# Layer 1 of a two-layer Mamba kernel: x turned by VectorE and laid out through DRAM instead of transposed on TensorE, with a new step order

## The chip, the cores and the metric

The kernel runs on one core of a Trainium2 chip, as one launch. The metric is the device time in microseconds, the median of several runs. Before the change the median of 3 runs is 8054.4 us (8048.22 to 8063.68).

## The reference

The input x is 2 images of 64 x 64 positions with 256 channels, in f32. Two layers follow each other, each as `x = x + layer(groupnorm(x))`. Layer 0 is a Mamba block with a scan over time. It runs in both directions along rows and along columns. Layer 1, which the change concerns, applies a Mamba-2 block four times (two stacked layers, each first along the columns and then along the rows). It treats every row or column of 64 positions as a sequence:

```python
def _mamba2(x, Win, Wconv, bconv, dt_bias, A_log, D, gn_w, Wout):
    zxbcdt = x @ Win
    z = zxbcdt[..., :DIN]
    xBC = silu(_causal_conv(zxbcdt[..., DIN:DIN + CONVDIM], Wconv, bconv))
    xh = xBC[..., :DIN].reshape(b, l, NHEADS, HEADP)
    Bm, Cm = xBC[..., DIN:DIN + DSTATE], xBC[..., DIN + DSTATE:]
    dt = softplus(zxbcdt[..., -NHEADS:] + dt_bias)
    A = -exp(A_log)
    y = _ssd(xh, dt, A, Bm, Cm) + rev(_ssd(rev(xh), rev(dt), A, rev(Bm), rev(Cm)))
    y = y + D[None, None, :, None] * xh
    return _rmsnorm(y.reshape(b, l, DIN) * silu(z), gn_w) @ Wout

# in _ssd:
    scores = einsum('bln,bsn->bls', Cm, Bm)[..., None] * decay * dt[:, None, :, :]
    return einsum('blsh,bshp->blhp', scores, xh)
```

DIN is 512, DSTATE 64, there are 8 heads of 64 channels and 4 convolution taps. Each application reads `x + _mamba2(_rmsnorm(x, w), ...)`.

## The kernel before

Channels lie on the 128 partitions and positions run along the free dimension. Both images stay in SBUF during layer 1 (`U[0]` and `U[1]`). Layer 1 is cut into 128 blocks: 4 calls (columns, rows, columns, rows) x 2 images x 16 blocks of 4 sequences, that is 256 positions per block (`TB`). `seq_view` gives a block its positions: contiguous for rows, strided for columns.

For one block the steps are these. `norm_squares`, `norm_total`, `norm_mean`, `norm_factor` and `norm_scale` make the RMS norm `xn`, 2 tiles of 128 channels by 256 positions. `x_proj` 0 and 1, `bc_proj`, `z_proj` 0 and 1 and `dt_proj` multiply `xn` with pieces of the weight `w_in` on TensorE. The 512 x channels are 4 tiles of 128 (`c`), two for each `x_proj`. `conv_start` (ScalarE) and `conv_taps` (VectorE, L1151) are the causal convolution, with the taps of each channel from `cols`. `dt_bias`, `dt_log` and `dt_sum` make softplus: an addition on VectorE (L1245), three activations on ScalarE (absolute value, exponential, logarithm) and a combination on VectorE (L1255). `dt_turn` transposes dt, and `factors` turns it into decay factors per head and position, writes them to DRAM (L1272) and reads them back broadcast over the partitions as `spread` (L1280). `decay_after` (L1290) and `decay_before` (L1296) make the decay matrices of both directions by two scans each on VectorE. `silus` activates x, z, B and C. `scores`, `scores_twice`, `weights` and `mix` form the 64 x 64 mixing matrices of each head, the last two on GpSimd. `outputs` multiplies them with x on TensorE, and for that x has to lie with positions on the partitions, as `xt`: `x_transpose` (L1332) does this with 8 transposes of 128 x 128 on TensorE into PSUM, and `x_copy` with 2 copies on ScalarE into SBUF. `gated` (L1410), `out_squares`, `out_total` (L1419), `out_mean`, `out_factor`, `out_proj`, `out_scale` (`res`, L1446) and `residual` (L1461) finish the block. In call 3 `y_load` (L1457) fetches the original input of the block, which `residual` adds before it stores the result (L1464).

The order is written out by hand in the table `STEPS`. Step n of block i is issued at the time 100 x i + the number in the table. All steps of all blocks, and the steps of `WEIGHTS` and `NORM`, are sorted by that time and emitted in this order:

```python
    return [
        (period * i + step[0], first + i, n, getattr(thing, step[1]), step[2:])
        for i, thing in enumerate(things)
        for n, step in enumerate(steps)
    ]
```

The numbers are no durations; only the order that they give counts. Since a block's last step stands at 533, some six blocks are in work at once. Compute instructions are pinned to this order, so each engine works through a fixed queue and waits at its head until the inputs of the next instruction are there. All DMAs of layer 1 go out on SP's queue, in order as well, though the framework may place them earlier or later among each other. PSUM has 7 banks for the blocks (`bank()`), which go round among the projections, scans, transposes, outputs and sums; a step that asks for one waits until an earlier user has been read. In SBUF the pools `one`, `two` and `three` hold one to three copies of a tile.

The weights of the four calls are loaded by `Weights.load` and scaled on VectorE by `scale_in` and `scale_out`; `decay_rates` makes `neg_a`. Image 1 is normalised during the first blocks (`NORM`).

Of the kernel before, what the change touches and what calls it, by code (L numbers as in the profile page):

```python
# [34 lines left out]
FAR = 1e35  # L35
UC = CT // 2
PARTS = P // TAPS
SPAN = L + TAPS - 1
WIDE = SB * SPAN
TURN = 1000  # L40
# [181 lines left out]

STEPS = (
    (0, "norm_squares"),
    (67, "norm_total"),
    (94, "norm_mean"),
    (104.4, "norm_factor"),
    (110.5, "norm_scale"),
    (149.4, "dt_proj"),
    (155.6, "x_proj", 0),  # L230
    (176.9, "conv_start", 0),
    (181.3, "bc_proj"),
    (184.4, "dt_bias"),
    (203.1, "bc_conv_start"),
    (206.9, "x_proj", 1),
    (207, "conv_taps", 0),
    (208.4, "dt_log"),
    (210.1, "conv_start", 1),
    (220.5, "dt_sum"),
    (226.2, "dt_turn"),  # L240
    (230.1, "factors"),
    (244.2, "z_proj", 1),
    (246.3, "conv_taps", 1),
    (249.4, "z_proj", 0),
    (274.9, "silus"),
    (292.8, "x_transpose", 0),
    (307.9, "x_copy", 0),
    (320.5, "scores"),
    (332.5, "scores_twice"),
    (348.9, "x_transpose", 1),  # L250
    (360, "weights", 0),
    (360.1, "weights", 1),
    (366.2, "decay_after", 0),
    (367.5, "decay_before", 0),
    (370.8, "decay_after", 1),
    (374.6, "x_copy", 1),
    (379, "mix", 0),
    (386.6, "decay_before", 1),
    (418.1, "mix", 1),
    (421.1, "outputs"),  # L260
    (433.8, "gated"),
    (445.2, "out_squares"),
    (458.9, "out_total"),
    (460.1, "out_mean"),
    (477, "out_proj"),
    (492.8, "out_factor"),
    (503.2, "out_scale"),
    (505, "y_load"),
    (533, "residual"),
)  # L270


# [1 line left out]
    (-1500, "load"),  # L274
    (10, "scale_in", 0),
    (20, "scale_in", 1),
    (200, "decay_rates"),
    (240, "diag_skip"),
    (300, "scale_out", 0),
    (330, "scale_out", 1),  # L280
# [748 lines left out]
def layer1(tc, k, d, U, kept, out):  # L1029
# [7 lines left out]
    with ExitStack() as ctx:  # L1037
# [4 lines left out]
        three = ctx.enter_context(tc.tile_pool(name="l1_three", bufs=3))  # L1042
        ps = ctx.enter_context(tc.tile_pool(name="l1_ps", bufs=7, space=PSUM))
        ps_one = ctx.enter_context(tc.tile_pool(name="l1_ps_one", bufs=1, space=PSUM))
        dram = ctx.enter_context(tc.tile_pool(name="l1_dram", bufs=3, space=bass.MemoryType.DRAM))
        pin = tc.keep_in_program_order

        k.more(nc, one)
# [17 lines left out]
        class Weights:  # L1066
# [97 lines left out]
        class Block:  # L1164
# [41 lines left out]
            def conv_start(self, h):  # L1206
                if not hasattr(self, "conv"):
                    self.conv = two.tile([P, CT, TB], F32, name="conv")
                for j in (1, 0):
                    c = 2 * h + j  # L1210
                    last_tap(self.conv[:, c, :], half_of(self.px[h], j), self.w.cols[:, c, :])

            def conv_taps(self, h):
                parts = [(self.conv[:, 2 * h + j, :], half_of(self.px[h], j), self.w.cols[:, 2 * h + j, :]) for j in range(2)]
# [46 lines left out]
            def factors(self):  # L1261
                a = factors[self.i % 2]
                for way, ls in enumerate((steps_up, steps_down)):
# [3 lines left out]
                        AF.Exp,  # L1267
                        scale=self.w.neg_a,
                    )
                rows = dram.tile([2, 2, NPAIR, NH, L], F32, name="factor_rows")  # L1270
                for q in range(NPAIR):
                    nc.sync.dma_start(  # L1272
                        out=rows[:, :, q].rearrange("e w h l -> h e w l"), in_=a[q * NH : (q + 1) * NH]
                    )
                self.spread = []
                for way in range(2):
                    to = three.tile([P, NPAIR, NH * L], F32, name="spread")
# [46 lines left out]
                pin(nc.scalar.preload_act_table_set(LOG_EXP))  # L1324


            def x_transpose(self, q):
                self.pt = getattr(self, "pt", {})
                self.pt[q] = bank()
                for c in range(CT):  # L1330
                    pin(
                        nc.tensor.transpose(  # L1332
                            self.pt[q][:, c * P : (c + 1) * P],
                            self.xh[:, c, q * P : (q + 1) * P],
                            k.ident,
                        )
                    )

            def x_copy(self, q):
                if not hasattr(self, "xt"):  # L1340
                    self.xt = two.tile([P, NPAIR, NH, DI // NH], F32, name="xt")
                act(self.xt[:, q].rearrange("p h e -> p (h e)"), self.pt[q], AF.Copy)


            def scores(self):
# [20 lines left out]

            def weights(self, q):
                self.weight = getattr(self, "weight", {})
                w = two.tile([P, NH, L], F32, name=f"weight{q}", tag=f"weight{q}")
                pin(  # L1370
                    nc.gpsimd.tensor_mul(
                        w,
                        self.score[:, q, :].unsqueeze(1).to_broadcast([P, NH, L]),
                        self.dt[:, q, :].unsqueeze(2).to_broadcast([P, NH, L]),
                    )
                )
                pin(nc.gpsimd.tensor_add(w, w, self.w.diag_d))
                self.weight[q] = w
# [1 line left out]


            def mix(self, q):
                self.mixes = getattr(self, "mixes", {})
                self.mixes[q] = two.tile([P, NH, L], F32, name=f"mix{q}", tag=f"mix{q}")
                decay = self.decay[q].rearrange("p (h l) -> p h l", l=L)
                pin(nc.gpsimd.tensor_mul(self.mixes[q], decay, self.weight[q]))


            def outputs(self):
# [3 lines left out]
                for q in range(NPAIR):  # L1393
                    for hd in range(NH):
                        for e, py in enumerate(self.py):
                            rows = slice(e * L, (e + 1) * L)
                            matmul(
                                py[(hd % 2) * L : (hd % 2 + 1) * L, hd // 2, q, :],
                                self.xt[rows, q, hd, :],
                                self.mixes[q][rows, hd, :],  # L1400
                                q == 0 and hd < 2,
                                q == NPAIR - 1 and hd >= NH - 2,
                            )
# [11 lines left out]
                act(self.sq2, self.yg, AF.Square)  # L1415

            def out_total(self):
                half = one.tile([P, 2, TB], F32, name="half2")
                pin(nc.gpsimd.tensor_add(half, self.sq2[:, 0:2, :], self.sq2[:, 2:4, :]))  # L1419
# [134 lines left out]
```

## Time and profile before

| what | value |
|---|---|
| median of 3 runs | 8054.4 us |
| time of the profiled execution | 8063.64 us |
| its span | 8061.9 us |
| first weight load of layer 1 | at 5973.63 us |
| busy in the span: TensorE matmul, VectorE, ScalarE, GpSimd | 7580.3, 7404.4, 7187.3, 6926.5 us |
| mean granted TensorE clock | 0.991 |
| DMA mean rate over the span | 141 GB/s |

The span runs from the first to the last instruction of the profiled execution, and the execution's own time lies 1.7 us above it. Busy time is the time in which an engine had an instruction running. In rows of groups and of the timeline, PE is the TensorE matmul, PEld its weight load, DVE is VectorE, ACT is ScalarE, POOL is GpSimd and SP the queue that issues the DMAs; L12 is line 12 of the kernel. An f32 matmul appears as two records, a transpose as one. Names are those of the program's tiles; every PSUM bank of `bank()` is called `ps_mm`.

### The profile page before, as it was taken

How to read it: one execution, taken by the hardware profiler on the slowest of the kernel's cores; microseconds unless marked ns; L12 is line 12 of the kernel's file. 1: busy time of each engine (PE TensorE's matmuls, PEld its weight loads, DVE VectorE, ACT ScalarE, POOL GpSimd, SP SyncE). 2: the span in 40 equal slices, each digit the busy share in tenths (PEclk: the TensorE clock that was granted, in tenths of full speed). 3: DMA queues.
4: the chain of work that ended last, by engine and by line, in shares of the span. 5: the costliest groups of instructions: out<-in, count | busy, mean ns of one | idle time of the engine just before them, and what ended most of it. 6: DMA issues, size and time to landing. Idle time of an engine off the chain costs nothing. (4 is left out here: it accounts for less than half of the span.)

```text
span 8061.9 us, 165546 instructions
## 1 busy us (share of the span) xinstructions
PE 7580.3 (94%) x62162; PEld 6487.4 (80%) x62162; DVE 7404.4 (92%) x6547; ACT 7187.3 (89%) x12867; POOL 6926.5 (86%) x3912
## 2 busy tenths in 40 slices
PE   7999999999999999999999999999979999999999
PEld 6888887888777778878887788888768888888887
DVE  6999999999999999999999999999988888888887
ACT  6999999999999989999999999999978888888887
POOL 6999999999998989999999999999867776677777
PEclk9999999999999999999999999999999999999999
DMA  5555556556555556555555555565532222222333
GB/s 173 165 163 161 165 161 169 165 166 168 161 169 163 163 158 172 163 166 159 161 165 162 175 166 164 168 169 172 152 105 67 68 78 68 76 70 68 82 102 93
DMA packets 703597, 1140.70 MB, mean 141 GB/s; under 512 B 121552, under 2 KB 269008, under 8 KB 701264
## 3 DMA queue, kind: packets, MB, share of 16 engines
q1 hardware_dynamic: 687296, 1110.54, 48.7%
q10 hardware_dynamic: 15504, 19.58, 0.8%
q8 instruction: 493, 8.08, 0.4%
q14 instruction: 304, 2.49, 0.1%
HBM read 1069.12 MB, written 60.69 MB: 140 GB/s over the span
## 5 line engine op out<-in xcount | busy, mean ns | idle before, releaser
L898 POOL TENSOR_TENSOR prod<-prod,c_row 128x1024 f32<-128x1024 f32 x1280 | 3011.3, 2368 | 420.5 <-DVE prod L887 250.3
L520 PE MATMUL ps_y<-ident,prod 128*128 128x128 f32 x16384 | 2129.5, 276 | 190.8 <-POOL prod L898 178.3
L520 PEld LDWEIGHTS ps_y<-ident,prod 128*128 128x128 f32 x16384 | 1828.5, 141 | 465.3 <-POOL prod L898 275.5
L868 POOL TENSOR_TENSOR b<-dtx,b_row 128x1024 f32<-128x1024 f32 x832 | 1960.1, 2370 | 22.5 <-DVE ps_h L887 11.2
L513 ACT ACTIVATE b<-dt,neg_a 128x512 f32<-128x512 f32 x2432 | 1591.5, 710 | 38.2 <-DVE ps_h L887 36.4
L513 ACT ACTIVATE scaled<-dtxt,bt 128x256 f32<-128x256 f32 x3328 | 1434.3, 496 | 80.8 <-PE ps_h L520 75.2
L887 DVE TENSOR_TENSOR_SCAN prod<-b,ps_h 128x1024 f32<-128x1024 f32 x640 | 1453.3, 2279 | 49.2 <-PE ps_h L520 40.3
L887 DVE TENSOR_TENSOR_SCAN prod<-ps_h,b 128x1024 f32<-128x1024 f32 x640 | 1437.2, 2272 | 57.5 <-ACT dbc L513 34.6
L887 DVE TENSOR_TENSOR_SCAN ps_h<-b,ps_h 128x1024 f32<-128x1024 f32 x576 | 1305.2, 2276 | 2.9 <-PE ps_h L516 1.9
L513 ACT ACTIVATE ps_h<-dt,neg_a 128x512 f32<-128x512 f32 x1664 | 1145.8, 689 | 147.1 <-DVE prod L901 60.7
L1064 PE MATMUL ps_mm<-xn,w_in 128*128 128x256 f32 x4608 | 1113.6, 383 | 0.0
L901 DVE TENSOR_TENSOR prod<-ps_h,c_row 128x1024 f32<-128x1024 f32 x768 | 931.3, 1220 | 123.6 <-PE ps_y L520 56.7
L1064 PEld LDWEIGHTS ps_mm<-xn,w_in 128*128 128x128 f32 x4608 | 849.1, 191 | 100.2
L520 PE MATMUL ps_h<-ident,scaled 128*128 128x128 f32 x6656 | 890.7, 276 | 36.2 <-DVE prod L887 22.4
L520 PEld LDWEIGHTS ps_h<-ident,scaled 128*128 128x128 f32 x6656 | 741.1, 141 | 179.6 <-ACT scaled L513 66.1
L516 PE MATMUL ps_h<-diag,dtxt 128*128 128x128 f32 x6144 | 771.9, 279 | 40.4 <-DVE prod L887 22.9
L516 PEld LDWEIGHTS ps_h<-diag,dtxt 128*128 128x128 f32 x6144 | 718.1, 192 | 88.6 <-DVE prod L887 53.8
L1151 DVE SCALAR_TENSOR_TENSOR conv<-ps_mm,cols,conv 128x252 f32<-128x252 f32 (+2 forms) x1536 | 630.8, 465 | 4.0 <-ACT conv L1061 4.0
L1419 POOL TENSOR_TENSOR half<-sq 128x512 f32<-128x512 f32 x128 | 163.0, 1274 | 529.9 <-ACT sq L1061 529.9
L516 PE MATMUL ps_mm<-xn,w_in 128*128 128x256 f32 x2048 | 502.5, 389 | 24.6 <-ACT dtxt L513 18.1
L513 ACT ACT_TABLE_LOAD x391 | 501.7, 1283 | 16.0 <-DVE prod L901 9.1
L1064 PE MATMUL ps_mm<-yg,w_out 128*128 128x256 f32 x2048 | 478.3, 387 | 14.3 <-DVE decay L1296 6.4
(145 smaller groups left out, 11714.8 us busy)
## 6 DMA issues: line engine op xcount, KB each, us to landing
c_row<-bc_rows SPq DMA_DIRECT2D x2048, 256.0 KB
b_row<-bc_rows SPq DMA_DIRECT2D x832, 256.0 KB
xs<-x_padded SPq DMA_DIRECT2D x1024, 134.0 KB
spread<-factor_rows SPq DMA_DIRECT2D x512, 256.0 KB
x_padded<-padded SPq DMA_DIRECT2D x128, 271.0 KB
y_in<-y SPq DMA_DIRECT2D x32, 256.0 KB
out_dram<-y_in SPq DMA_DIRECT2D x32, 256.0 KB
XU<-in_x_dram SPq DMA_DIRECT2D x8, 512.0 KB
```

The costliest lines, as they stand in the source:

```text
L513: pin(nc.scalar.activation(*args, **kwargs))
L516: pin(nc.tensor.matmul(out, lhsT=lhsT, rhs=rhs, start=start, stop=stop))
L520: nc.tensor.matmul(out, lhsT=x, rhs=order, start=start, stop=stop, is_transpose=True)
L868: pin(nc.gpsimd.tensor_mul(b, self.dtx[u], self.over_tiles(u, 0, n)))
L887: nc.vector.tensor_tensor_scan(*(t.rearrange("p c t -> p (c t)") for t in (to, a, b)), 0.0, ALU.mult, ALU.add,)
L898: pin(nc.gpsimd.tensor_mul(prod, prod, self.over_tiles(u, 1, n)))
L901: pin(nc.vector.tensor_mul(prod, self.h[u, n], self.over_tiles(u, 1, n)))
L1064: pin(nc.tensor.matmul(out, lhsT=lhsT, rhs=rhs, start=start, stop=stop))
L1151: nc.vector.scalar_tensor_tensor(to, seqs(pp)[:, :, : L - j], w[:, TAPS - 1 - j : TAPS - j], to, ALU.mult, ALU.add,)
L1419: pin(nc.gpsimd.tensor_add(half, self.sq2[:, 0:2, :], self.sq2[:, 2:4, :]))
```

## The change

The x channels are dealt to the four tiles in groups of 32. Tile c now holds, on partitions 32a to 32a + 31, the channels 128a + 32c and up. For this `Weights.load` fetches the x part of `w_in` in eight DMAs that permute the columns, the rest in two, and a second copy of the taps, `x_cols`, in four.

`x_turn` is one VectorE transpose of the whole activated x, 128 x 1024, which transposes each square of 32 x 32 by itself. `x_out` writes the result to DRAM in four DMAs, and `x_in` reads it back in one, with positions on the partitions and the channels in their natural order. `x_transpose` and `x_copy` are gone.

`mix` writes its product into the weight's buffer, of which there are now three instead of two copies. `out_total` adds in place, and `y_in` has one copy instead of two. `factors` is cut in two: the spreads become a step of their own. The pool of DRAM tiles has 4 copies instead of 3. `STEPS` has new numbers throughout, and `decay_rates` moves from 200 to 60.

```diff
 STEPS = (
     (0, "norm_squares"),
...
+    (97.6, "norm_scale"),
+    (106.3, "dt_proj"),
+    (121.1, "x_proj", 0),
+    (141.4, "dt_bias"),
+    (146, "conv_start", 0),
+    (146.1, "dt_log"),
+    (146.6, "dt_sum"),
+    (146.8, "dt_turn"),
+    (149.6, "factors"),
+    (202.3, "x_proj", 1),
+    (202.4, "bc_proj"),
+    (206.3, "conv_start", 1),
+    (206.4, "bc_conv_start"),
+    (229.1, "conv_taps", 1),
+    (236.6, "z_proj", 1),
+    (236.7, "z_proj", 0),
+    (254.2, "conv_taps", 0),
+    (282.8, "silus"),
+    (288.3, "scores"),
+    (290.5, "x_turn"),
+    (292.7, "scores_twice"),
+    (321.1, "spreads"),
+    (331.7, "x_out"),
+    (333.1, "weights", 0),
+    (333.2, "weights", 1),
+    (370.4, "decay_after", 0),
+    (378.6, "decay_before", 0),
+    (379.7, "decay_after", 1),
+    (399.9, "decay_before", 1),
+    (402.8, "x_in"),
+    (402.9, "mix", 0),
+    (439.9, "mix", 1),
+    (460, "outputs"),
+    (470.4, "gated"),
+    (506.4, "out_squares"),
+    (554.7, "out_total"),
+    (571, "out_proj"),
+    (575.4, "out_mean"),
+    (589.8, "out_factor"),
+    (600, "out_scale"),
+    (605, "y_load"),
+    (646, "residual"),
 )
...
-    (200, "decay_rates"),
+    (60, "decay_rates"),
...
-        dram = ctx.enter_context(tc.tile_pool(name="l1_dram", bufs=3, space=bass.MemoryType.DRAM))
+        dram = ctx.enter_context(tc.tile_pool(name="l1_dram", bufs=4, space=bass.MemoryType.DRAM))
...
-                nc.sync.dma_start(out=self.w_in, in_=d[self.ax + "_Win"][self.li])
+                src = d[self.ax + "_Win"][self.li]
+                for kt in range(KT):
+                    to, by = (w[:, kt, DI : 2 * DI] for w in (self.w_in, src))
+                    to = to.rearrange("p (c a j) -> p c a j", c=CT, j=SQ)
+                    by = by.rearrange("p (a c j) -> p c a j", c=CT, j=SQ)
+                    for c in range(CT):
+                        nc.sync.dma_start(out=to[:, c], in_=by[:, c])
+                for part in (slice(0, DI), slice(2 * DI, PROJ)):
+                    nc.sync.dma_start(out=self.w_in[:, :, part], in_=src[:, :, part])
...
+                self.x_cols = wp.tile([P, CT, TAPS + 1], F32, name="x_cols")
+                src = d[self.ax + "_cols"][self.li][:, :, : TAPS + 1]
+                for a in range(CT):
+                    nc.sync.dma_start(
+                        out=self.x_cols[a * SQ : (a + 1) * SQ],
+                        in_=src[:, a, :].rearrange("(c j) n -> j c n", j=SQ),
+                    )
...
-            def x_transpose(self, q):
...
-            def x_copy(self, q):
...
+            def x_turn(self):
+                self.turned = two.tile([P, TB // SQ, CT, SQ], F32, name="turned")
+                pin(
+                    nc.vector.transpose(
+                        self.turned.rearrange("p b c j -> p c b j"),
+                        self.xh.rearrange("p c (b i) -> p c b i", i=SQ),
+                    )
+                )
+
+            def x_out(self):
+                self.xd = dram.tile([TB, P // SQ, CT * SQ], F32, name="x_turned")
+                for a in range(P // SQ):
+                    nc.sync.dma_start(
+                        out=self.xd[:, a, :].rearrange("(b i) w -> i b w", i=SQ),
+                        in_=self.turned[a * SQ : (a + 1) * SQ].rearrange("p b c j -> p b (c j)"),
+                    )
+
+            def x_in(self):
+                self.xt = two.tile([P, NPAIR, NH, DI // NH], F32, name="xt")
+                nc.sync.dma_start(
+                    out=self.xt.rearrange("p q h e -> p q (h e)"),
+                    in_=self.xd.rearrange("(q p) a w -> p q (a w)", q=NPAIR),
+                )
...
-                w = two.tile([P, NH, L], F32, name=f"weight{q}", tag=f"weight{q}")
+                w = three.tile([P, NH, L], F32, name=f"weight{q}", tag=f"weight{q}")
...
-                self.mixes = getattr(self, "mixes", {})
-                self.mixes[q] = two.tile([P, NH, L], F32, name=f"mix{q}", tag=f"mix{q}")
                 decay = self.decay[q].rearrange("p (h l) -> p h l", l=L)
-                pin(nc.gpsimd.tensor_mul(self.mixes[q], decay, self.weight[q]))
+                pin(nc.gpsimd.tensor_mul(self.weight[q], decay, self.weight[q]))
...
-                    self.y = two.tile([P, KT, TB], F32, name="y_in")
+                    self.y = one.tile([P, KT, TB], F32, name="y_in")
```

In the built program, one block's worth of VectorE's queue, once every stage is filled, reads: `res`, nine taps (`conv_taps` 1 with B and C), `dt_bias`, `dt_sum`, six taps (`conv_taps` 0), two `gated`, `decay_after` 0, `decay_before` 0, `decay_after` 1, `x_turn`, `scores_twice`, `norm_scale`, `decay_before` 1.

More of the change, by code (lines that the diff above doesn't have):

```diff
@@ L37 @@
 PARTS = P // TAPS
+SQ = 32
 SPAN = L + TAPS - 1
@@ L224 @@
     (0, "norm_squares"),
[L225 to L269, printed above, removed]
+    (46.6, "norm_total"),
+    (75.4, "norm_mean"),
+    (85.7, "norm_factor"),
+    (97.6, "norm_scale"),
[6 more added lines that the diff above has]
+    (146.8, "dt_turn"),
@@ L1210, in conv_start @@
                     c = 2 * h + j
-                    last_tap(self.conv[:, c, :], half_of(self.px[h], j), self.w.cols[:, c, :])
+                    last_tap(self.conv[:, c, :], half_of(self.px[h], j), self.w.x_cols[:, c, :])
             def conv_taps(self, h):
-                parts = [(self.conv[:, 2 * h + j, :], half_of(self.px[h], j), self.w.cols[:, 2 * h + j, :]) for j in range(2)]
+                parts = [(self.conv[:, 2 * h + j, :], half_of(self.px[h], j), self.w.x_cols[:, 2 * h + j, :]) for j in range(2)]
                 if h:
@@ L1269, in factors @@
                     )
-                rows = dram.tile([2, 2, NPAIR, NH, L], F32, name="factor_rows")
+                rows = self.rows = dram.tile([2, 2, NPAIR, NH, L], F32, name="factor_rows")
                 for q in range(NPAIR):
@@ L1274, in factors, with spreads @@
                     )
+            def spreads(self):
+                rows = self.rows
                 self.spread = []
@@ L1324, in bc_silu @@
                 pin(nc.scalar.preload_act_table_set(LOG_EXP))
-            def x_transpose(self, q):
[L1328 to L1336, printed above, removed]
-                    )
-            def x_copy(self, q):
-                if not hasattr(self, "xt"):
-                    self.xt = two.tile([P, NPAIR, NH, DI // NH], F32, name="xt")
-                act(self.xt[:, q].rearrange("p h e -> p (h e)"), self.pt[q], AF.Copy)
+            def x_turn(self):
[4 more added lines that the diff above has]
+                        self.xh.rearrange("p c (b i) -> p c b i", i=SQ),
+                    )
+                )
[12 more added lines that the diff above has]
+                )
             def scores(self):
@@ L1399, in outputs @@
                                 self.xt[rows, q, hd, :],
-                                self.mixes[q][rows, hd, :],
+                                self.weight[q][rows, hd, :],
                                 q == 0 and hd < 2,
@@ L1417, in out_total @@
             def out_total(self):
-                half = one.tile([P, 2, TB], F32, name="half2")
-                pin(nc.gpsimd.tensor_add(half, self.sq2[:, 0:2, :], self.sq2[:, 2:4, :]))
+                half = self.sq2[:, 0:2, :]
+                pin(nc.gpsimd.tensor_add(half, half, self.sq2[:, 2:4, :]))
                 self.total2 = two.tile([P, TB], F32, name="total2")
```

## The prediction

> **What bounds the kernel now.** I read the engine totals first, then the engines in two stretches of layer 1, then the chain of work that ended last inside layer 1, and only then single groups.
>
> ```profile
> PE 7580.3 (94%) x62162; PEld 6487.4 (80%) x62162; DVE 7404.4 (92%) x6547; ACT 7187.3 (89%) x12867; POOL 6926.5 (86%) x3912
> ```
>
> The totals mix two layers. The change touches layer 1 alone, which starts at 5973.6 us (the first weight load) and takes 2088 us. Its instructions in layer 0 stand in the same order as before, so layer 0 counts as nothing here. Next, two stretches of layer 1 (columns: stretch, length, busy time of PE, PEld, DVE, ACT, POOL, granted clock, DMA share, GB/s):
>
> ```profile
> 6528.30:6987.30 459.00, 455.06 (x4196) 390.25 (x4195) 388.10 (x754) 376.60 (x724) 317.53 (x290) 1.00 0.26 70
> 7018.90:7493.80 474.90, 471.70 (x4322) 404.55 (x4325) 412.72 (x782) 401.18 (x750) 339.26 (x300) 1.00 0.27 70
> ```
>
> The stretches hold 29 and 30 blocks, 15.83 us each. The first lies in call 1 (sequences along the rows of the image, contiguous), the second in call 2 (along its columns, strided). Per block TensorE is busy 15.7 us of 15.83, VectorE 13.38 in the first and 13.76 in the second, ScalarE 13.0 and 13.4, GpSimd 11.0 and 11.3. DMA takes a quarter. TensorE is full; VectorE has 2.1 to 2.4 us per block to spare. The chain (start, length) shows the loop that repeats each 15.83 us:
>
> ```profile
> 7952.22 3.65 PE ps_mm L1064 x82
> 7955.87 1.27 DVE yg L1410 x2
> 7957.14 0.78 DVE conv L1151 x2
> 7958.30 0.77 DVE conv L1151 x2
> 7960.51 1.23 DVE ps_mm L1290
> 7961.76 1.23 DVE decay L1296
> 7963.03 4.58 PE ps_mm L1064 x20
> ```
>
> `outputs` on TensorE releases `gated` on VectorE; taps and scans stand behind it, and the last scan frees the PSUM bank of `out_proj`. So TensorE's full queue and this loop end nearly together. The groups that the change removes, and VectorE's one large idle time (last columns: busy us, mean ns, idle before):
>
> ```profile
> L1332 PE MATMUL ps_mm<-ident,xh 128*128 128x128 f32 x804 | 120.6, 273 | 0.0
> L1332 PEld LDWEIGHTS ps_mm<-ident,xh 128*128 128x128 f32 x804 | 100.5, 141 | 20.3
> L1061 ACT ACTIVATE xt<-ps_mm 128x512 f32<-128x512 f32 x202 | 120.1, 595 | 0.1
> L1446 DVE TENSOR_TENSOR res<-ps_mm,rms 128x512 f32<-128x512 f32 x100 | 69.1, 691 | 196.4 <-ACT rms L1061 194.4 <-PE ps_mm L1064 2.0
> ```
>
> **What is removed.** Eight transposes per block. Each group of four holds TensorE's queue for about 0.5 us (0.44 by the start of the next matmul, 0.57 by the weight loads), so 1.0 us per block: TensorE's floor falls from 15.7 to 14.7. ScalarE loses two copies, 1.1 us; it waits for others already, so nothing comes of it.
>
> **What is added on VectorE: the turn.** One transpose of 128x1024 f32 per block. No such operation is in the trace. The nearest row has the same number of f32 elements:
>
> ```profile
> L901 DVE TENSOR_TENSOR prod<-ps_h,c_row 128x1024 f32<-128x1024 f32 x768 | 931.3, 1220 | 123.6 <-PE ps_y L520 56.7
> ```
>
> 1.22 us recorded, and 1.13 us of queue, since neighbours in this trace start 0.08 to 0.09 us before the recorded end of the one ahead. From below: 0.6 us, if it ran as fast as the weight scaling of 128x1160 (0.81 us at L1106). From above: 2.3 us, if it cost twice as much per element, as the scans do (1.21 us for 512 at L1290). [...] 2.3 stays for the range.
>
> **What the new order adds: a stall.** Before, `dt_bias` (184.4) and `dt_sum` (220.5) have taps and a scan between them. Now they are at 141.4 and 146.6, and in the built order nothing lies between them on VectorE. `dt_sum` needs three ScalarE operations that need `dt_bias`:
>
> ```profile
> 6518.16 0.16 DVE L1245 TENSOR_TENSOR dt<-ps_mm,bias 128x16 f32<-128x16 f32 x1
> ...
> 6523.91 0.20 ACT L1061 ACTIVATE ps_mm<-dt 128x16 f32<-128x16 f32 x1
> 6524.14 0.17 ACT L1061 ACTIVATE ps_mm<-ps_mm 128x16 f32<-128x16 f32 x1
> 6524.34 0.25 ACT L1061 ACTIVATE ps_mm<-ps_mm,one 128x16 f32<-128x16 f32 x1
> ...
> 6525.09 0.16 DVE L1255 SCALAR_TENSOR_TENSOR dt<-dt,ps_mm 128x16 f32<-128x16 f32 x1
> ```
>
> 0.16 for `dt_bias`, 0.03 of handover, 0.68 on ScalarE (6523.91 to 6524.59), 0.03 back: 0.90 instead of 0.12 until the next start, so VectorE loses 0.78 us per block. Queued behind `dt_sum` are six taps, and behind these the activation of x, `gated` and the scans. ScalarE itself should be ready: its preceding activation needs `x_proj` 0, which TensorE finishes over 1.5 us earlier.
>
> **The sum per block.** VectorE's own work without the once-per-call scaling is 13.28 in calls 1 and 3; in calls 0 and 2 the strided `norm_scale` costs 0.38 more (1.06 against 0.68 us), so 13.66. Adding 1.13 and 0.78: 15.19 and 15.57. Both exceed TensorE's 14.7, so VectorE becomes the bound and its 2 us wait before `res` goes. I walked the other queues against a 15.2 us period. ScalarE has about 12 us. GpSimd keeps 11; the product written into the weight's buffer changes no size. `out_factor` is done 2 us before `res` wants it, `mix` 1 about 1 us before `outputs` does. The tightest is `bc_conv_start`, 0.4 us before its tap. Gain: 64 x (15.83 - 15.19) + 64 x (15.83 - 15.57) = 41 + 17 = 58 us.
>
> **Moved and hidden: the trip through DRAM.** SP gets four stores and one load more per block, 1 MB in all. Its cycle is: one spread load, `x_in`, three spreads, four `x_out`, two `factors`. `x_in` waits for the stores to land, and holds three spreads behind it. But the stores go out right after the turn, at the period's end, SP then waits for `factors` some 6 us into the next one, and `x_in` comes after that; its data are wanted 13 us later, at `outputs`. Spreads are wanted 10 us after issue. The layout costs nothing while it stays inside these margins; if a load came 1 us late each block, that would be 128 us. The DMA share rises from 0.26 to about 0.45, still under half. The fourth DRAM buffer, the third weight buffer, the split of `spreads` from `factors` and the two PSUM banks fewer per block (15 for 17) only loosen waits: nothing.
>
> **Costs paid once.** (a) The start: now two lines set it.
>
> ```profile
> 5980.29 1.56 DVE L1106 TENSOR_SCALAR w_in<-w_in,norm_w 128x1160 f32<-128x1160 f32 x2 [4.91 <-DMA norm_w<-in_L_t_norm_w_dram]
> ...
> 5982.96 1.01 DVE L1191 TENSOR_TENSOR xn<-XU,ps_mm 128x512 f32<-128x512 f32 x1 [1.11 <-issue]
> ```
>
> The first call's `load` issues 13 more DMAs at about 0.4 us, eight of them in runs of 128 bytes, and `decay_rates` (200, now 60) stands ahead of the first `norm_scale` on VectorE and ahead of its factor on ScalarE, waiting for `neg_a`, one of the last loads. I add 7 us (4 to 12). Later loads are a dozen blocks early: nothing. (b) Weight scaling (4.6 us per call) and the 16 statistics of image 1 (0.6 us each) lay partly in VectorE's slack; with none left they cost about 13 us more. (c) The end: the pipeline is one block deeper, but the tail after the last `norm_scale`, 59 us now, walks to about the same: 0, give or take 5. The single `y_in` buffer lets load and store follow each other 6 us or more apart: nothing.
>
> **Total.** -58 + 7 + 13 = -38 us. The profiled execution took 8063.6 us around a span of 8061.9, 9 us above the median; its sum gives 8026, and from the median 8054.4 I get **8016 us**. Changes under 0.2% (16 us) can't be told from none.
>
> **Rivals.**
> *A, VectorE bound, turn at 1.1 to 1.3 us (55%):* 7995 to 8038.
> *B, the turn costs 2.3 us (15%):* VectorE 16.4 and 16.7, so 8016 + 128 x 1.17 = 8166, slower. It decides alone: from 1.43 us for the turn (1.13 + 38/128) the gain is gone, from 1.55 the kernel is slower. [...] Against: L901.
> *C, the DRAM trip or the deeper dependencies are late by 0.3 to 0.6 us per block (12%):* 8054 to 8093. Against: the margins above; for: SP holds everything in one queue.
> *D, VectorE cheaper than thought (turn at 0.6 us, or the stall filled) (10%):* then TensorE's 14.7 plus some friction bounds, 7950 to 7985.
> *E, the transposes go, but other exposed waits eat the gain (8%):* 8038 to 8070. That the transposes stay on TensorE is excluded: they are not in the built program.
>
> **The numbers.** Faster: most of A and D, 0.62. Same: E and parts of A and C, 0.13. Slower: B and most of C, 0.25. The range runs from D's middle to beyond C: 7965 to 8105, leaving out B and half of D. A's own range is 7995 to 8038.
>
> **What would show it.** TensorE busy 14.7 us per block and no L1332-like transposes; VectorE over 94% busy in the stretches of layer 1; the transpose row at 1.2 us; a wait of VectorE for ScalarE of about 0.8 us before each `dt_sum`, 128 times; next to none before `res`; a period of 15.2 in calls 1 and 3 and 15.6 in 0 and 2. Wrong if the transpose row reads above 1.4 us, if `outputs` waits for the load of x, or if scans wait for spreads.

## The result, and the profile after

The changed kernel takes 8061.3 us (median of 20 runs), the kernel before 8053.4 us in the runs beside them. The ratio is 1.0008, with a 95% interval from 1.0001 to 1.0015: a loss of 0.08%, where 8016 us and a clear gain were forecast. The prediction's range, 7965 to 8105, holds the result, but only because it is wide enough for its unlikely cases. What came is rival E, which had 8%: the transposes are gone and the gain is eaten elsewhere.

The profiled execution of the changed kernel spans 8048.3 us. Its layer 1 begins at 5953.67 us, 20 us sooner than in the profiled execution of before, although the instructions ahead of it stand in the same order; in the profiles of the other runs it begins anywhere between 5955 and 5980 us. So layer 1 is compared by itself, from the first weight load to the end of the span: 2094.6 us against 2088.3, 6.3 us longer, which agrees with the ratio. Engine totals of the kernel after:

```profile
PE 7481.2 (93%) x61138; PEld 6389.6 (79%) x61138; DVE 7555.7 (94%) x6675; ACT 7067.0 (88%) x12613; POOL 6929.8 (86%) x3912
```

TensorE lost 99 us and VectorE gained 151. Two stretches of 27 undisturbed blocks of the kernel after, in calls 1 and 2 (stretch, length, busy time of PE, PEld, DVE, ACT, POOL, granted clock, DMA share, GB/s):

```profile
6555.05:6973.43 418.38, 405.64 (x3705) 345.41 (x3704) 391.19 (x730) 325.03 (x622) 296.07 (x271) 1.00 0.52 140
7055.35:7479.15 423.80, 405.64 (x3705) 345.41 (x3704) 400.97 (x730) 335.81 (x622) 305.47 (x271) 1.00 0.51 138
```

A block takes 15.50 us in call 1 (418.38 / 27) and 15.70 us in call 2; it took 15.83 in both. The forecast was 15.19 and 15.57. TensorE is busy 15.02 us per block; 14.7 was forecast. VectorE is busy 14.49 and 14.85. The clock is full in both, so it plays no part. The groups that answer to those of before (busy us, mean ns, idle before), from 6300 to 7900 us:

```profile
L1349 DVE STREAM_TRANSPOSE turned<-xh 128x1024 f32<-128x1024 f32 x101 | 123.1, 1219 | 0.0
L1271 DVE SCALAR_TENSOR_TENSOR dt<-dt,ps_mm 128x16 f32<-128x16 f32 x102 | 17.5, 171 | 74.9 <-ACT ps_mm L1062 74.9
L1470 DVE TENSOR_TENSOR res<-ps_mm,rms 128x512 f32<-128x512 f32 x102 | 67.3, 660 | 0.0
```

The turn is 1.22 us recorded, the wait before `dt_sum` is 0.73 us and comes every time, and the old wait before `res` is gone: all three as forecast. One block of call 1 in the timeline of the kernel after (start, length, idle before):

```profile
6701.87 0.17 DVE L1261 TENSOR_TENSOR dt<-ps_mm,bias 128x16 f32<-128x16 f32 x1
...
6702.77 0.17 DVE L1271 SCALAR_TENSOR_TENSOR dt<-dt,ps_mm 128x16 f32<-128x16 f32 x1 [0.73 <-ACT ps_mm L1062]
6702.86 2.39 DVE L1167 SCALAR_TENSOR_TENSOR conv<-ps_mm,x_cols,conv 128x252 f32<-128x252 f32 x6
...
6705.30 3.72 PE L1065 MATMUL ps_mm<-yg,w_out 128*128 128x256 f32 x16 [0.48 <-DVE conv L1167]
...
6709.29 0.59 PE L1065 MATMUL ps_mm<-total,mean_c 128*128 128x256 f32 x2
...
6709.93 0.45 ACT L1062 ACTIVATE ps_mm<-ps_mm,eps_rms 128x256 f32<-128x256 f32 x1 [0.18 <-PE ps_mm L1065]
...
6712.23 1.02 ACT L1062 ACTIVATE conv<-ps_mm,x_cols 128x256 f32<-128x256 f32 x2 [0.16 <-PE ps_mm L1065]
6713.14 1.05 ACT L1062 ACTIVATE sq<-yg 128x1024 f32<-128x1024 f32 x1
6713.63 0.85 DVE L1167 SCALAR_TENSOR_TENSOR conv<-ps_mm,x_cols,conv 128x252 f32<-128x252 f32 x2
...
6714.09 0.56 ACT L1062 ACTIVATE conv_bc<-ps_mm,bc_cols 128x256 f32<-128x256 f32 x1
...
6714.69 0.48 DVE L1167 SCALAR_TENSOR_TENSOR conv_bc<-ps_mm,bc_cols,conv_bc 128x252 f32<-128x252 f32 x1 [0.21 <-ACT conv_bc L1062]
```

From `dt_bias` to `dt_sum` are 0.90 us, as worked out. But there is a second wait. The tap of B and C starts 1.06 us after the two taps ahead of it start, where 0.77 would do: it waits 0.29 us for `bc_conv_start`, which ScalarE reaches only after `out_squares` (6713.14). Read backwards, ScalarE is late because `norm_factor` waited for `mean_c`, that stands behind `out_proj` on TensorE, and `out_proj` waited 0.48 us for the last tap of `conv_taps` 0, which frees its PSUM bank. That tap is on VectorE, behind `dt_sum`. So VectorE, TensorE and ScalarE hang in one loop. This way back is read from the rows. The run below that takes the wait out tests what it costs, not each link.

The account of layer 1:

| part | forecast | measured | how |
|---|---|---|---|
| undisturbed blocks | -58 | -29.9 | 64 x (15.83 - 15.495) + 63 x (15.83 - 15.696) |
| start, first load to first `xn` | +7 | +9.1 | 18.44 against 9.33 |
| blocks with once-per-call work, filling of the pipeline included | +13 | +21.8 | first to last `xn` less 127 periods: 30.4 against 8.6 |
| end, from the last `xn` | 0 | +5.4 | 65.3 against 59.9 |
| sum | -38 | +6.4 | |

The start, in the kernel after:

```profile
5964.81 1.56 DVE L1122 TENSOR_SCALAR w_in<-w_in,norm_w 128x1160 f32<-128x1160 f32 x2 [9.38 <-DMA x_cols<-in_L_t_cols_dram]
...
5968.37 0.20 ACT L1062 ACTIVATE neg_a<-neg_a 16x1 f32<-16x1 f32 x1 [10.80 <-DMA neg_a<-in_L_t_heads_dram]
...
5972.11 1.01 DVE L1207 TENSOR_TENSOR xn<-XU,ps_mm 128x512 f32<-128x512 f32 x1 [3.36 <-ACT ps_mm L1062]
```

ScalarE stands 10.8 us behind the load of `neg_a`, and the factor of the first norm behind it. At the end, the chain of work that ended last (start, length) runs through GpSimd, where the last blocks queue: two sums, into the image and the result, stand ahead of the `out_total` that the block behind needs. In the kernel after:

```profile
8027.42 1.27 POOL Y L1485
...
8028.77 1.27 POOL y_in L1487
8030.05 1.24 POOL sq L1443
```

But the kernel before ends in the same way:

```profile
8042.86 1.27 POOL Y L1461
8044.20 1.26 POOL y_in L1463
...
8046.21 1.27 POOL half L1419
```

So this queue does not explain the 5.4 us more at the end; their cause stays open.

### The profile page after: what moved, and what is told of

It is laid out like the page before. It is cut to its first block, busy times and chain, and to the rows that moved or that the text cites. A ratio compares the mean times of both kernels' runs of the same rounds, so it can differ in the third digit from the quotient of the medians.

```text
span 8048.3 us, 164212 instructions
## 1 busy us (share of the span) xinstructions
PE 7481.2 (93%) x61138; PEld 6389.6 (79%) x61138; DVE 7555.7 (94%) x6675; ACT 7067.0 (88%) x12613; POOL 6929.8 (86%) x3912
## 5 line engine op out<-in xcount | busy, mean ns | idle before, releaser
L1065 PE MATMUL ps_mm<-xn,w_in 128*128 128x256 f32 x4608 | 1069.0, 386 | 1.8 <-ACT rms L1062 1.8
L902 DVE TENSOR_TENSOR prod<-ps_h,c_row 128x1024 f32<-128x1024 f32 x768 | 931.6, 1220 | 111.4 <-PE ps_y L521 44.3
L1410 POOL TENSOR_TENSOR weight<-decay,weight 128x512 f32<-128x512 f32 x256 | 325.8, 1273 | 364.5 <-DVE decay L1315 364.5
L1167 DVE SCALAR_TENSOR_TENSOR conv<-ps_mm,x_cols,conv 128x252 f32<-128x252 f32 (+2 forms) x1536 | 631.1, 466 | 2.8 <-ACT conv L1062 2.6
L517 PE MATMUL ps_mm<-xn,w_in 128*128 128x256 f32 x2048 | 500.2, 388 | 24.3 <-ACT dtxt L514 17.6
```

Source lines behind the costliest of these rows:

```text
L517: pin(nc.tensor.matmul(out, lhsT=lhsT, rhs=rhs, start=start, stop=stop))
L902: pin(nc.vector.tensor_mul(prod, self.h[u, n], self.over_tiles(u, 1, n)))
L1065: pin(nc.tensor.matmul(out, lhsT=lhsT, rhs=rhs, start=start, stop=stop))
L1167: nc.vector.scalar_tensor_tensor(to, seqs(pp)[:, :, : L - j], w[:, TAPS - 1 - j : TAPS - j], to, ALU.mult, ALU.add,)
L1410: pin(nc.gpsimd.tensor_mul(self.weight[q], decay, self.weight[q]))
```

## The experiments

Four questions: does VectorE's queue, stall included, set the new period; does the order or the turn cost the gain; what set the old period; and what was the wait for `bc_conv_start` worth. Times are medians, beside the kernel before in the same batch of runs. Only the run that says so leaves out a part of the computation.

**The stall taken out, first try.**

```diff
-    (141.4, "dt_bias"),
+    (128, "dt_bias"),
```

> Theory S (the stall in front of dt_sum sits on VectorE's queue, and this queue sets the period of the changed kernel): with dt_bias ahead of the nine taps of conv_taps 1, the three ScalarE operations of dt_log run beside the taps and 0.78 us per block go. Periods fall from 15.50 and 15.69 to 14.8 to 14.9, near TensorE's 14.7; in all 128 x 0.7 to 0.8, so 90 to 100 us less than the changed kernel: 7965 (7945 to 7990). Rival L (a loop over several engines, or the trip through DRAM, sets the period, and VectorE's wait only shows it): the wait moves to another place, less than 20 us come of it: over 8040.

8048.6 us beside 8061.3 (0.9982, interval 0.9970 to 0.9994). By its number this is rival L, but the waits of this kernel from 6300 to 7900 us (total us, times, longest) name another cause:

```profile
DVE dt L1261 <- POOL weight L1397: 100.8, 99, 1.2
```

The stall before `dt_sum` is gone, but `dt_bias`, now earlier, waits 1.0 us for a buffer of `dt`. There are two copies, and GpSimd's `weights` still reads the older one. The period is 15.5 in all calls. The run decided nothing and was repeated with a third copy.

**The stall taken out, with three copies of dt.**

```diff
-    (141.4, "dt_bias"),
+    (128, "dt_bias"),
...
-                self.dt = two.tile([P, NPAIR, NH], F32, name="dt")
+                self.dt = three.tile([P, NPAIR, NH], F32, name="dt")
```

> The same move of dt_bias as in the run before, with three copies of dt instead of two, because there the moved dt_bias waited 1.0 us per block for GpSimd to finish reading the older copy. Theory S (VectorE's queue, with the stall in it, sets the period of the changed kernel): no wait is left in VectorE's queue but that for conv_bc; its sum is 14.4 us in calls 1 and 3 and 14.8 in 0 and 2, TensorE has 14.7, so the periods are 14.7 to 15.0 and the time 7965 (7950 to 7990). Rival L (a loop over several engines sets the period in any case): the wait moves again, over 8030.

8001.9 us beside 8060.5: 0.9923 (0.9908 to 0.9938). The windows of 25 and 24 blocks:

```profile
6579.16:6954.35 375.19, 375.19 (x3427) 317.77 (x3426) 359.47 (x676) 295.40 (x576) 274.71 (x250) 1.00 0.55 146
7092.74:7454.16 361.42, 360.59 (x3290) 306.29 (x3289) 353.64 (x650) 295.02 (x553) 272.75 (x240) 1.00 0.54 144
```

15.01 and 15.06 us per block, at the slow end of what theory S gave, and TensorE is busy in every microsecond of the first. So the stall and what it delayed held the changed kernel; without it TensorE bounds, at 15.0 us. Layer 1 is 70.6 us shorter than in the changed kernel, and the periods give as much: 64 x (15.495 - 15.01) + 63 x (15.696 - 15.06) = 71. The time misses the expected 7950 to 7990 by 12 us, since the expectation still took TensorE at 14.7. The third copy has nothing to take away by itself: in the changed kernel `dt_bias` does not wait for a buffer.

**The other wait of VectorE.** Two neighbours on ScalarE exchange places:

```diff
-    (206.4, "bc_conv_start"),
+    (206.35, "bc_conv_start"),
```

> The changed kernel with two neighbours on ScalarE exchanged: bc_conv_start (206.4, now 206.35) ahead of out_squares, so that conv_bc is there about 1 us sooner. If the loop from the last tap of conv_taps 0 over out_proj, the means and ScalarE to the bc tap is what makes the period 15.50 instead of VectorE's own 15.2 in calls 1 and 3, the 0.29 us before the bc tap goes there: period 15.2, in calls 0 and 2 still 15.7, and the time is 64 x 0.29 = 18 us less than the changed kernel, about 8043. If the wait is only the place where something else shows (TensorE at 15.0 plus its own waits, or squares late for out_total), the period stays at 15.5 and the time at 8055 to 8065.

8024.0 us beside 8044.3: 0.9971 (0.9961 to 0.9982). The windows of 27 blocks each:

```profile
6553.08:6963.67 410.59, 405.67 (x3701) 345.48 (x3700) 388.91 (x730) 324.63 (x622) 296.00 (x270) 1.00 0.51 142
7045.31:7465.26 419.95, 405.65 (x3701) 345.48 (x3700) 398.27 (x731) 334.68 (x622) 305.41 (x270) 1.00 0.49 139
```

15.21 and 15.55 us per block. These are the prediction's 15.19 and 15.57: its sum of VectorE's queue was right, and the place where it failed is this wait. VectorE now waits only for `dt_sum`, 0.73 us per block, and twice 0.03 us between scans, so its queue with the stall in it is the whole period. The other wait was worth 0.29 us in calls 1 and 3, and 0.14 in calls 0 and 2, where the expectation had none. Layer 1 of the profile is 25.6 us shorter than in the changed kernel.

**The turn made twice.** 
```diff
-                pin(
-                    nc.vector.transpose(
...
+                for _ in range(2):
+                    pin(
+                        nc.vector.transpose(
```

> The changed kernel with the turn made twice into the same tile. It gives the price of a turn where it stands. If VectorE's queue sets the period and a turn takes 1.14 us of it: 128 x 1.0 to 1.14, so 8185 to 8210. If the loop over out_proj and ScalarE sets it in calls 1 and 3, where VectorE waits 0.3 us for conv_bc, the second turn costs 0.85 there: 8185 to 8190. If the period hangs on something else, as the trip through DRAM: under 8120.

8204.2 us beside 8060.5: 1.0175 (1.0160 to 1.0190). Layer 1 is 133 us longer than in the changed kernel, 1.04 us for each of the 128 second turns. VectorE's time is paid nearly in full, so the turn is on the path that sets the period: 8204 lies in the range given for VectorE's queue. Calls 1 and 3, at 16.5 us, pay 1.0, not the 0.85 that the wait for `conv_bc` would leave, so that wait does not take up a longer queue. No turn of the 256 is over 1.25 us recorded.

**The old order with the new path of x.**

```diff
+    (230.2, "spreads"),
...
-    (292.8, "x_transpose", 0),
-    (307.9, "x_copy", 0),
+    (292.8, "x_turn"),
+    (292.9, "x_out"),
...
-    (348.9, "x_transpose", 1),
+    (348.9, "x_in"),
...
-    (374.6, "x_copy", 1),
```

> The changed kernel with the old step order: the turn where x_transpose 0 was, the stores right behind it, the load where x_transpose 1 was, spreads right behind factors. No stall of dt. By the prediction's way of counting (VectorE 13.3 to 13.7 and 1.1 for the turn, TensorE 14.7) the period is 14.8 and the time 7930 to 7960. If the closed loop of VectorE and ScalarE (15.9 us: res to the end of conv_taps 1, then silus to out_factor) set the old period, the turn falls into the wait before res, the period stays at 15.8, and the time is 8045 to 8070 with the later start. If the turn or the trip through DRAM is dearer than it looks, over 8080.

8079.1 us beside 8061.3: 1.0017 (1.0008 to 1.0026), above the 8070 that the loop allowed, by 9 us, of which the slower batch makes 7. The period is 15.83 in all calls, to 0.01 the old one, although TensorE is busy 0.6 us less and VectorE has 1.14 more to do. The turn fell into VectorE's wait before `res`, which was 196 us from 6300 to 7900 us and is here:

```profile
L1470 DVE TENSOR_TENSOR res<-ps_mm,rms 128x512 f32<-128x512 f32 x101 | 69.7, 690 | 91.0 <-ACT rms L1062 91.0
```

So half of VectorE's wait was to spare for the turn, which cost the period nothing there, and TensorE's lighter load gained nothing.

**The kernel before without its transposes.** `x_copy` copies the activated x as it lies, so x is untransposed and the outputs are not those of the reference.

```diff
-                self.pt[q] = bank()
-                for c in range(CT):
-                    pin(
-                        nc.tensor.transpose(
...
+                self.pt[q] = self.xh[:, 2 * q : 2 * q + 2, :].rearrange("p c t -> p (c t)")
```

> The kernel before without its eight transposes per block: x_copy copies the untransposed x from SBUF at the same place on ScalarE, so that x is wrong in the outputs; everything else stays. If TensorE's 15.7 us per block set the old period, as the prediction said, it falls to 14.8 to 15.0: 7930 to 7970. If the closed loop of VectorE (res to the last tap of conv, 8.6 us) and ScalarE (table load, silus, table load, conv_start, out_factor, 7.1 us) set it, the period stays at 15.8: 8040 to 8062.

8059.6 us beside 8060.5: 0.9995 (0.9987 to 1.0004). A window of 26 blocks in call 1:

```profile
6556.88:6968.55 411.67, 392.63 (x3562) 333.33 (x3562) 346.70 (x678) 334.96 (x651) 284.48 (x260) 1.00 0.26 69
```

TensorE is busy 15.10 us of 15.83, 0.6 less than before, and the period is the old one to 0.01. TensorE's work did not set it. The loop in the timeline of this kernel:

```profile
6704.23 0.84 DVE L1151 SCALAR_TENSOR_TENSOR conv<-ps_mm,cols,conv 128x244 f32<-128x244 f32 x2
...
6705.15 1.28 ACT L1061 ACT_TABLE_LOAD   x1 [1.53 <-DVE conv L1151]
...
6706.44 1.06 ACT L1061 ACTIVATE xh<-conv 128x1024 f32<-128x1024 f32 x1
...
6709.20 1.28 ACT L1324 ACT_TABLE_LOAD   x1
...
6710.49 1.02 ACT L1061 ACTIVATE conv<-ps_mm,cols 128x256 f32<-128x256 f32 x2
...
6711.89 0.38 ACT L1061 ACTIVATE rms<-ps_mm 128x256 f32<-128x256 f32 x1
...
6712.30 0.69 DVE L1438 TENSOR_TENSOR res<-ps_mm,rms 128x512 f32<-128x512 f32 x1 [2.09 <-ACT rms L1061]
...
6712.91 2.38 DVE L1151 SCALAR_TENSOR_TENSOR conv<-ps_mm,cols,conv 128x252 f32<-128x252 f32 x6
...
6715.35 1.16 PE L1064 MATMUL ps_mm<-mix,xt 64*64 64x64 f32 x62 [0.23 <-DVE conv L1151]
...
6716.54 1.29 DVE L1402 TENSOR_TENSOR yg<-ps_mm,gate 128x512 f32<-128x512 f32 x2 [0.38 <-PE ps_mm L1064]
```

VectorE's last taps of x release ScalarE, which then works without a gap for 7.1 us (6705.15 to 6712.27) through two table loads, the activations, `conv_start` and `out_factor`; that releases `res`, and behind `res` on VectorE stand the taps, `dt_sum` and `gated` up to the last taps, 8.6 us. In between the loop passes over TensorE: `outputs` waits for the bank that the taps free, and `gated` waits 0.38 us for `outputs`. Together 15.8 us, the period, and VectorE's wait of 2.1 us before `res` runs beside ScalarE's part.

**A stall put into the kernel before.**

```diff
-    (184.4, "dt_bias"),
-    (208.4, "dt_log"),
+    (220.3, "dt_bias"),
+    (220.4, "dt_log"),
     (220.5, "dt_sum"),
```

> The kernel before, with dt_bias and dt_log moved up to dt_sum, so that the same stall arises in the old order. If VectorE's 2 us of waiting before res were slack, as the prediction read them, the stall of 0.9 us disappears in it: 8054 to 8070. If they belong to a closed loop (res, taps, yg, taps on VectorE, 9.0 us by the trace; then silus, conv_start and out_factor on ScalarE, 6.9 us; 15.9 together, which is the period), there is no slack and the stall is paid in full: 128 x 0.78 to 0.9, so 8150 to 8170.

8127.5 us beside 8061.3: 1.0070 (1.0053 to 1.0086), between the two expectations. The period is 16.29, 0.46 more. From the waits of this kernel, 6300 to 7900 us:

```profile
PE ps_mm L1259 <- DVE dt L1255: 58.6, 98, 1.8
```

And from its timeline:

```profile
6714.78 1.28 ACT L1061 ACT_TABLE_LOAD   x1
...
6715.26 0.84 DVE L1151 SCALAR_TENSOR_TENSOR conv<-ps_mm,cols,conv 128x244 f32<-128x244 f32 x2
...
6716.13 1.06 ACT L1061 ACTIVATE xh<-conv 128x1024 f32<-128x1024 f32 x1
```

Here `dt_turn` waits 0.60 us on TensorE for the late `dt_sum`, and 15.7 + 0.6 is the new period. So TensorE's 15.7 us was a second bound, 0.13 us below the loop. But the edit changed the loop as well: the table load ahead of `silus` starts here before the last taps of x, while in the old order it waits for them (6705.15 in the rows above), so 1.28 us left the loop as the stall came in. The run therefore does not show what a stall inside the old loop costs.

**Opening the loop**, by one move, in the old order with the new path and in the kernel before:

```diff
-    (503.2, "out_scale"),
...
-    (533, "residual"),
+    (533, "out_scale"),
+    (533.1, "residual"),
```

> The changed kernel in the old order, as in the run e4, with out_scale alone moved: from 503.2, where it waits for rms and holds the taps behind it, to 533, behind taps, dt_sum and scores_twice. If the closed loop set the period of 15.83 there, it now runs over conv_start instead of rms (0.9 us less) and without the first res in it (0.6 us taken from ahead of the taps, given back behind them), about 14.9 us; then TensorE's queue sets the period, 15.0 us as in the run with three copies of dt: 7975 to 8005. If the loop was not what held e4 (but the turn, the trip through DRAM or TensorE), it stays at 8070 to 8085.

> The kernel before with the same single move of out_scale. The loop opens here too, but TensorE still has its transposes, 15.7 us per block: 0.05 to 0.13 us per block come of it, 8044 to 8055. If the loop alone counted and TensorE had room, it would fall as far as the run e11: under 8000. If the move closes another loop, over 8065.

The first took 8049.5 us beside 8053.3: 0.9998 (0.9989 to 1.0006), the second 8059.7: 1.0013 (1.0005 to 1.0021). Both miss their expected times, and the periods say why. In calls 1 and 3 they fell from 15.83 to 15.30 (15.44 in most of call 3) and to 15.74; in calls 0 and 2 they rose to 16.07 and 16.09. The first half is the loop theory's: with the transposes on TensorE there are 0.09 us to gain, without them 0.53 (0.9 were expected; by the trace the loop that is left, over `conv_start`, holds 0.3 us of waiting for TensorE, above all for `scores`, which the expectation left out). The second half was overlooked: in calls 0 and 2 `norm_squares` and `norm_scale` read strided, take 0.5 and 0.3 us longer (1.12 for 0.62 and 1.02 for 0.69 in the first kernel), and with `res` out of the way the taps run so early that VectorE then waits for `norm_factor`, as this row of call 2 in the first kernel shows:

```profile
7110.89 1.02 DVE L1207 TENSOR_TENSOR xn<-XU,ps_mm 128x512 f32<-128x512 f32 x1 [0.57 <-ACT ps_mm L1062]
```

That the strided reads close this second loop is read from the trace and was not tested by itself.

**The new order with the old path of x.** The transposes stand at 290.5 and 345, the copies at 310 and 372; these places were chosen for this run.

> The new step order with the old path of x: transposes on TensorE, copies on ScalarE, x channels in their old places, one load of w_in. TensorE is back at 15.7 us per block, VectorE at 14.4 with the stall. If TensorE's floor then sets the period: 15.8, and the time is that of the kernel before or a little over, 8045 to 8075. If the loop through out_proj's bank and ScalarE sets it, with two copies of 0.6 us on ScalarE in it: 16.1 to 16.5, so 8090 to 8150.

8173.0 us beside 8061.3: 1.0124 (1.0107 to 1.0141), above both expectations, period 16.6. TensorE is busy 16.2 us of it, although the same matmuls were busy 15.7 in the old order, so its busy time depends on the order too. VectorE waits at five places per block of call 1 (`yg` 0.8, `dt_sum` 0.73, `conv_bc` 0.5, the taps of x 0.4, `xn` 0.3 us), and no single cause was isolated. A better placing of the copies might do better, so this run shows only that the new order is no good place for the old path as it stands.

**Four edits at once.**

```diff
-    (141.4, "dt_bias"),
+    (128, "dt_bias"),
...
-    (506.4, "out_squares"),
+    (546.05, "out_squares"),
...
-    (60, "decay_rates"),
+    (120, "decay_rates"),
...
-                self.dt = two.tile([P, NPAIR, NH], F32, name="dt")
+                self.dt = three.tile([P, NPAIR, NH], F32, name="dt")
```

> The changed kernel with dt_bias ahead of conv_taps 1, three copies of dt, out_squares behind bc_conv_start on ScalarE (so that the bc tap is not late), and decay_rates moved behind the first norm_scale. By theory S 64 x 0.2 at most comes from out_squares and 2 to 4 us from decay_rates on top of the run with dt alone: 7950 (7935 to 7980), bounded by TensorE's 14.7 us. If another loop closes: no faster than that run.

8033.6 us beside 8060.5: 0.9965 (0.9952 to 0.9977), slower than with `dt` alone and far from the expected 7950. Its waits from 6300 to 7900 us:

```profile
DVE dt L1271 <- ACT ps_mm L1062: 65.8, 97, 0.7
```

The stall is back: 546.05 puts `out_squares`, 1.05 us, directly ahead of `dt_log` on ScalarE, so the three operations end after the nine taps that should cover them. The start is 12.5 instead of 18.4 us.

**Three of the four edits.** The same without the move of `out_squares`:

```diff
-    (141.4, "dt_bias"),
+    (128, "dt_bias"),
...
-    (60, "decay_rates"),
+    (120, "decay_rates"),
...
-                self.dt = two.tile([P, NPAIR, NH], F32, name="dt")
+                self.dt = three.tile([P, NPAIR, NH], F32, name="dt")
```

> The changed kernel with dt_bias ahead of conv_taps 1, three copies of dt, and decay_rates moved from 60 to 120, behind the first norm_scale. Against the run with three copies of dt alone, the start is 5 to 6 us shorter (18.2 to 12.5 us from the first weight load to the first norm_scale, as in the run with four edits): 7996 (7988 to 8003). If the start is hidden behind a later load: 8002.

7989.7 us beside 8053.3: 0.9926 (0.9913 to 0.9940). It is faster than both kernels. TensorE is busy 390.11 of 390.11 us in a stretch of 26 blocks, so in this order it has no idle time left. The start is 12.5 us, as expected, and in the profiles layer 1 is 6.0 us shorter than with three copies of `dt` alone (2018.0 against 2024.0). The ratios of the two runs, 0.9926 and 0.9923, do not show a gain that small.

## Why the prediction was wrong

*What bounds the kernel.* "TensorE is full; VectorE has 2.1 to 2.4 us per block to spare." TensorE was full, but its work did not set the period: without the transposes the old kernel keeps its 15.83 us. The loop that the prediction named, over the bank of `out_proj`, was not the one that closed: that was `res` to the last taps, then ScalarE up to `rms`. The row that the prediction showed, `res` waiting 196 us in total for ScalarE's `rms`, was the loop's own mark, and ScalarE was not followed back from it. Of VectorE's wait, 1.1 us did take up the turn in the old order, yet counting busy times as the prediction did gave a period of 14.8 for that run, and 15.83 came. This error alone did not spoil the number: the old period was measured and not derived, and for the new order the prediction had walked `out_factor` and found it early enough for `res`, by 2 us (1.5 in the trace), so that loop is open there.

*What is removed.* 1.0 us per block on TensorE was forecast, 0.67 came (15.69 to 15.02 busy), and 0.59 where only the transposes went. Mis-sized; VectorE bounds the changed kernel, so this costs nothing there, but it is why rival D's 7950 was out of reach even with the stall filled.

*The turn.* 1.13 us of queue was forecast, 1.14 start to start; the second turn cost 1.04. The row of L901 was the right neighbour: the turn takes 1.22 us recorded (1219 ns), as L901 does for as many elements (1220 ns). The price per element of the scans, 1.21 us for 512, would have doubled it; of the 128 turns none is over 1.245 us. Rival B is out.

*The stall.* 0.90 us from `dt_bias` to `dt_sum`, right to 0.01.

*The sum per block.* **This is the step that failed**: "The tightest is `bc_conv_start`, 0.4 us before its tap." It held up its tap by 0.29 us in calls 1 and 3 and by 0.14 in calls 0 and 2. 64 x 0.29 + 64 x 0.14 is 28 us, all that the undisturbed blocks fell short. With the wait taken out, 15.21 and 15.55 came, against 15.19 and 15.57. By the rows of call 1, the prediction left out that `out_proj` waits for its bank and holds up what stands behind it on TensorE: ScalarE waits there 0.18 us for `mean_c` and 0.16 for `x_proj` 1. That is 0.34 of the 0.7 us between 0.4 early and 0.29 late; where the rest of the margin went is not shown.

*The DRAM trip.* Hidden, as forecast. TensorE's rows from 6300 to 7900 us show no wait for `xt`, and the whole run two, 4.4 us together; no scan waits for a spread. The DMA share is 0.52, where 0.45 was forecast. The half of rival C that names the DRAM trip is out. Its other half, late dependencies, is close to what came, with 0.29 and 0.14 us per block instead of 0.3 to 0.6.

*Costs paid once.* Start +9.1 for +7, once-per-call work +21.8 for +13, end +5.4 for 0: 16 us together, three misses in the same direction. Moving `decay_rates` took back 5.7 us of the start (18.2 to 12.5, with three copies of `dt` in both). Of the once-per-call work one part is seen: scaling `w_in` took 1.52 us each instead of 0.81 (below), 4 us for six. The rest of it and the end were not tested.

Together, 28 and 16 us are the 44 us between -38 and +6. That VectorE's queue becomes the bound, the turn and the stall were right. A margin called tight was taken at its estimated sign, and it made the larger part of the miss; the costs paid once made the rest.

## What to carry to other kernels

A full engine is not yet the bound, and another engine's wait can belong to a loop: follow the wait back through every engine until it closes or leaves the period, before calling anything the bound, and test it by leaving the suspected bound's work out. Work put into such a wait can be free, as the turn was in the old order, and still nothing gets faster. When an engine becomes the bound, each near-tie on its queue has to be costed with both signs, and two edits that are good alone can meet in one queue. An operand moved earlier needs a buffer that is free earlier.

## What the hardware showed

VectorE's scaling of 128 x 1160 in f32 takes 0.81 to 0.82 us in all eight places of the kernel before; at 7493.10 us, for one, GpSimd has nothing to do from 7492.63 to 7498.25. In the kernel after it falls beside GpSimd's work:

```profile
7482.97 1.04 POOL L1397 TENSOR_TENSOR weight<-score,dt 128x512 f32<-128x512 f32 x1
7483.14 3.25 DVE L1122 TENSOR_SCALAR w_in<-w_in,norm_w 128x1160 f32<-128x1160 f32 x2
7484.09 1.67 POOL L1403 TENSOR_TENSOR weight<-weight,diag_d 128x512 f32<-128x512 f32 x1
7485.72 1.79 POOL L1410 TENSOR_TENSOR weight<-decay,weight 128x512 f32<-128x512 f32 x1
```

Two scalings take 3.25 us instead of 1.62, and GpSimd's sum and product 1.67 and 1.79 instead of 1.27 each. So both engines are slower in these rows, where they work side by side. Why is not shown: no run here isolates it.
